# Weight loads of an attention kernel: five transfers at once, or six parts over six tiles

## The chip, the cores and the metric

The kernel runs on one core of a Trainium2 chip. The metric is the device time of one execution in microseconds (us), the median of several runs. The profile comes from one execution, taken by the hardware profiler. A kilobyte (KB) is 1024 bytes.

## The reference

One layer on x of 2048 rows by 256: attention with 16 heads of 128, and then a mixture of experts. Every projection matrix is stored as codes with one scale per block of 32 rows.

```
w  = codes * repeat(scales, 32, axis=0)        # wq, wk, wv: 256 x 2048; wo: 2048 x 256
q, k, v = ln(x) @ w + bias                     # 16 heads of 128
attn = softmax(q k^T / sqrt(128)); out = attn @ v
x = x + ln(out @ wo + bo)
x = x + ln(top-2 of 8 experts: silu(x Wg) * (x Wu) @ Wd)
```

## The kernel before

The attention stage is one loop over 256 steps, `g = 16 * h + t`: head `h` and tile `t`, a block of 128 query rows. The order of the instructions on each engine is the order of the program text; the framework adds only the semaphore waits.

In one tile, the steps are these.

- TensorE multiplies Q by K^T for the 2048 keys in two halves (L453 to L457). Every operand is split into a high and a low float16 part, so three products stand for one.
- VectorE takes the row maxima (L458), and ScalarE the exponential with its row sums (L469).
- VectorE forms the reciprocal of the row sum (L479, once per tile), and ScalarE writes the normalized high part `ph` (L483).
- VectorE writes the low part `pl` in two halves (L498), from `p`, `m` and `ph`.
- SP, the queue of the sync engine, transposes `ph` (L486) and `pl` (L502) into `pt` with one DMA each. There are two buffers of `pl`, three of `ph`, and two of `pt`, each for four tiles.
- TensorE multiplies V by `pt` (L517 to L519), some six tiles later: `PVLAG` counts in half tiles. After four tiles the result `o` is scaled by ScalarE, split into two float16 parts by POOL (GpSimd, L531 and L532) and written to `ot_d` in DRAM by POOL's DMA queue (L533, 256 KB). This comes in tiles 2, 6, 10 and 14 of each head.

Between these, `fill` projects Q, K and V of the coming heads, a piece in each tile: ScalarE takes a piece out of PSUM (L204, L235), and POOL splits it (L205 and L206, L236 and L237). POOL works through its queue in order, so that a split of tile t often runs in tile t + 1.

The weights are used in pairs of heads, p = h // 2: 256 columns of `wq`, `wk` and `wv` each. `load_w` brings one of them: four transfers of 64 KB for the scales, each row repeated over 32 partitions (L130), and one of 256 KB for the codes (L135), all issued on POOL's queue, into the tiles `st_s` and `st_c`, of which there is one each. `dequant` scales the scales (L152) and multiplies (L154) on POOL. For pair p + 1 this goes on in the even head of pair p: V, K and Q are loaded in tiles 0, 3 and 6, at the beginning of the tile, and dequantized in tiles 2, 5 and 8. Odd heads load nothing.

In head 14, the last even one, three of the eight loads of `wo` take the place of these: `load_wo` in tiles 7, 10 and 13 issues four transfers of scales on ScalarE's queue (L571) and the codes on SP's (L576); `dequant_wo` (L584) follows in tiles 9, 12 and 15. The other five come in head 15, from `late`. After the attention stage come the output projection and the experts.

Of the kernel before, what the change touches and what calls it, by code (L numbers as in the profile page):

```python
# [8 lines left out]
F32 = mybir.dt.float32  # L9
# [12 lines left out]
D = 256  # L22
NH = 16
# [14 lines left out]
def sandwich(  # L38
# [22 lines left out]
    nc = tc.nc  # L61
# [53 lines left out]
    stage = proj_ctx.enter_context(tc.tile_pool(name="stage", bufs=1, side="right"))  # L115

    W = {}
    raw = {}

    def load_w(p, which, pool, eng, sbufs=1):  # L120
        codes, scales = {
            "q": (wq_codes, wq_scales),
            "k": (wk_codes, wk_scales),
            "v": (wv_codes, wv_scales),
        }[which]
        cols = bass.ts(p, 256)
        sc = pool.tile([128, 2, 256], F32, name="st_s", bufs=sbufs)
        sv = scales.rearrange("(kc b) n -> b kc n", b=4)
        for b in range(4):
            eng.dma_start(  # L130
                out=sc[32 * b : 32 * b + 32],
                in_=sv[b : b + 1, :, cols].to_broadcast([32, 2, 256]),
            )
        cd = pool.tile([128, 2, 256], F32, name="st_c", bufs=sbufs)
        eng.dma_start(  # L135
            out=cd, in_=codes.rearrange("(kc p) n -> p kc n", p=128)[:, :, cols]
        )
        raw[(p, which)] = (sc, cd)

    IX = {"q": 0, "k": 1, "v": 2}  # L140

# [6 lines left out]
    def dequant(p, which):  # L148
        sc, cd = raw.pop((p, which))
        f = sig[:, 2, IX[which] : IX[which] + 1]  # L150
        if p > 0:
            nc.gpsimd.tensor_scalar(sc, sc, f, 1.0, ALU.mult, ALU.mult)  # L152
        w = wpool.tile([128, 2, 256], BF, name="w" + which)
        nc.gpsimd.tensor_tensor(w, cd, sc, ALU.mult)  # L154
        W[(p, which)] = w
# [18 lines left out]
    def flush():  # L174
        while pending:
            pending.pop(0)()
# [32 lines left out]
    def proj_v(p, t0, n, tag="pj", wide=None):  # L209
        w = W[(p, "v")]  # L210
        ps = proj_psum(tag)
        for j in range(n):
            i = 0
            for kc in range(2):
                for hl in range(2):
                    nc.tensor.matmul(
                        ps[:, bass.ts(j, 256)], xnT[:, t0 + j, hl * 2 + kc, :],
                        w[:, kc, :], start=(i == 0), stop=(i == 3),
                    )
                    i += 1  # L220
        if t0 % 4 == 0:
            V[(p, t0 // 4)] = kqv.tile([128, 2, 4, 256], HP, name="v", bufs=7)
        v = V[(p, t0 // 4)]
        sl = slice(t0 % 4, t0 % 4 + n)
        psv = ps[:, : n * 256].rearrange("p (t d) -> p t d", d=256)
        if wide is None:
            nc.scalar.copy(v[:, 0, sl, :], psv)
            pending.append(lambda: nc.vector.tensor_tensor(
                v[:, 1, sl, :], psv, v[:, 0, sl, :], ALU.subtract
            ))  # L230
        else:
            t32 = wide.tile([128, 512], F32, name="t32")[:, : n * 256].rearrange(
                "p (t d) -> p t d", d=256
            )
            nc.scalar.copy(t32, psv)  # L235
            nc.gpsimd.tensor_copy(v[:, 0, sl, :], t32)  # L236
            nc.gpsimd.tensor_tensor(v[:, 1, sl, :], t32, v[:, 0, sl, :], ALU.subtract)  # L237

    with tc.tile_pool(name="start", bufs=4) as st:
# [9 lines left out]
        for i, scales in enumerate((wq_scales, wk_scales, wv_scales)):  # L249
            nc.scalar.dma_start(  # L250
                out=smax[:, i], in_=scales.rearrange("b (c n) -> (b c) n", n=128)
            )
        for i, bias in enumerate((bq, bk, bv)):
            nc.scalar.dma_start(
                out=b48[16 * i : 16 * i + 16], in_=bias.rearrange("(h p) -> h p", p=128)
            )
        cds = {}
        for i, (which, codes, scales) in enumerate(
# [3 lines left out]
            cd = st.tile([128, 2, 256], F32, name="cd0", bufs=3)  # L262
            nc.sync.dma_start(
                out=cd, in_=codes.rearrange("(kc p) n -> p kc n", p=128)[:, :, 0:256]
# [182 lines left out]
    def scores_half(h, t, half, m):  # L447
        q = Q[(h, t // 4)]
        qc = bass.ts(t % 4, 128)
        s = s_pair()  # L450
        for j in range(2):
            k = K[(h, 2 * half + j)]
            nc.tensor.matmul(s[:, j, :], q[:, 0, qc], k[:, 0, :], start=True, stop=False)  # L453
            nc.tensor.matmul(s[:, j, :], q[:, 0, qc], k[:, 1, :], start=False, stop=False)  # L454
        for j in range(2):
            k = K[(h, 2 * half + j)]
            nc.tensor.matmul(s[:, j, :], q[:, 1, qc], k[:, 0, :], start=False, stop=True)  # L457
        nc.vector.tensor_reduce(m[:, half : half + 1], s, AX.XY, ALU.max)  # L458
        return s
# [15 lines left out]
    def recip(m):  # L475
        nc.vector.tensor_scalar(
            m[:, 5:6], m[:, 3:4], m[:, 4:5], 1.0 / PS, ALU.add, ALU.mult
        )
        nc.vector.reciprocal(m[:, 6:7], m[:, 5:6])  # L479
# [76 lines left out]
    def pv_unit(u):  # L556
        n, e = divmod(u - PVLAG, 8)
        if 0 <= n < 4 * NH:
            pv_part(n // 4, n % 4, 2 * e, 2 * e + 2)
# [3 lines left out]
    so = wo_scales.rearrange("(h b) n -> b h n", b=4)  # L563
    co = wo_codes.rearrange("(h p) n -> p h n", p=128)
    wo_raw = {}

    def load_wo(j, pool, tags, bufs):
        hs = slice(2 * j, 2 * j + 2)
        sc = pool.tile([128, 2, D], F32, name="wos", tag=tags[0], bufs=bufs)
        for b in range(4):  # L570
            nc.scalar.dma_start(  # L571
                out=sc[32 * b : 32 * b + 32],
                in_=so[b : b + 1, hs].to_broadcast([32, 2, D]),
            )
        cd = pool.tile([128, 2, D], F32, name="woc", tag=tags[1], bufs=bufs)
        nc.sync.dma_start(out=cd, in_=co[:, hs])  # L576
        wo_raw[j] = (sc, cd)

    def dequant_wo(j):
        sc, cd = wo_raw.pop(j)  # L580
        if j % 4 == 0:
            wo.append(kqv.tile([128, 8, D], BF, name="wo", tag="v", bufs=7))
        hs = slice(2 * (j % 4), 2 * (j % 4) + 2)
        nc.gpsimd.tensor_tensor(wo[j // 4][:, hs], cd, sc, ALU.mult)  # L584
# [43 lines left out]
    def load_oi(b, half, j, tag="kT"):  # L628
        oi = kqv.tile(
            [128, 4, 2, 256], HP, name="oi", tag=tag, bufs={"kT": 8, "v": 7}[tag]  # L630
        )
        nc.sync.dma_start(
            out=oi, in_=ot_d[b][:, 4 * j : 4 * j + 4, :, bass.ts(half, 256)]
        )
        OIN[(b, half, j)] = oi
# [40 lines left out]
    for g in range(NS + 2):  # L676
        h, t = divmod(g, NT)
        live = g < NS
        if live:
            if t in (0, 3, 6) and h % 2 == 0 and h + 2 < NH:  # L680
                load_w(h // 2 + 1, "vkq"[t // 3], stage, nc.gpsimd)
            m = small.tile([128, 8], F32, name="m", bufs=6)
            s0 = scores_half(h, t, 0, m)
            if g == 0:
                proj_v(0, 0, 2)
                proj_v(0, 2, 2, "pv")
        if g == NS:
            load_oi(0, 1, 1)
            load_oi(0, 1, 2)
            load_oi(0, 1, 3)  # L690
        if prev is not None:
            recip(prev[2])
        if prev2 is not None:
            low_half(1, *prev2)
        flush()
        if defer:
            pv_unit(2 * g - 1)
            defer = False
        pv_unit(2 * g)
        if prev is not None:  # L700
            prev = (*prev, high_part(*prev))
        if live:
            s1 = scores_half(h, t, 1, m)
            negmax(m)
            p = softmax((s0, s1), m)
        if prev is not None:
            low_half(0, *prev)
        prev2 = prev
        first = live and (2 * g + 1 - PVLAG) % 8 == 0
        if not first:  # L710
            pv_unit(2 * g + 1)
        if live:
            fill(h, t)
        if first and h == NH - 1:
            defer = True
        elif first:
            pv_unit(2 * g + 1)
        if live:
            prev = (h, t, m, p)
        else:  # L720
            prev = None
        if h % 2 == 0 and t in (2, 5, 8) and h + 2 < NH:
            dequant(h // 2 + 1, "vkq"[t // 3])
        if h == 0 and t in (8, 9):
            tail_consts(t - 8)
        if h == NH - 2 and t in (7, 10, 13):
            load_wo((t - 7) // 3, stage, ("st_s", "st_c"), 1)
        if h == NH - 2 and t in (9, 12, 15):
            dequant_wo((t - 9) // 3)
        if h == NH - 1:  # L730
            late(t)
        if g == NS:
            X1[0] = kqv.tile([128, 4, D], F32, name="x1_0", tag="kT", bufs=8)
            nc.sync.dma_start(out=X1[0], in_=XV[:, 0])
# [377 lines left out]
    for q in range(4 * NCH + 2):  # L1112
        b, c = divmod(q, NCH)
# [61 lines left out]
```

## Time and profile before

| | us |
|---|---|
| median of 3 runs | 1877.07 |
| lowest and highest | 1873.67 and 1882.77 |
| the profiled execution | 1879.05 |
| its span, first to last instruction | 1877.3 |
| the loop over heads: first and last `L479` | 38.9 and 1588.5 |

The page of the profile gives for each engine the busy time, its share of the span and the number of instructions. Its digits are busy tenths in 40 slices of the span. The share of the DMA engines can pass 1.00, since packets overlap. In a row of the timeline, a transfer that an engine issues has the time that the issue took, not the time to its landing. A wait is told as "engine, line <- what ended it: us in total, times, longest". In a table of stretches, each row is a stretch of time with the busy time of each engine and its number of instructions, the granted clock of TensorE, the DMA share, and GB/s.

### The profile page before, as it was taken

The numbers are of one execution on the slowest core, as the hardware profiler recorded it, in microseconds if no ns is written. First come the engines' busy times: TensorE is split into PE (matmuls) and PEld (weight loads), VectorE is DVE, ScalarE is ACT, GpSimd is POOL, SyncE is SP. The second block draws the span as 40 slices with busy tenths as digits, with TensorE's granted clock in tenths as the row PEclk, the third lists the DMA queues.
The fourth block names the chain that finished last, engine by engine and source line by source line (L and its number), as shares of the span: only waits on it lengthen the run. The fifth ranks groups of instructions, "written<-read, shape, count | busy, mean of one in ns | idle before, by whom it ended". The sixth has DMA issues, their size and how long they took to land. (4 is left out here: it accounts for less than half of the span.)

```text
span 1877.3 us, 25533 instructions
## 1 busy us (share of the span) xinstructions
PE 1794.1 (96%) x8890; PEld 936.0 (50%) x8890; DVE 1632.4 (87%) x2267; ACT 1365.5 (73%) x1730; POOL 907.5 (48%) x893
## 2 busy tenths in 40 slices
PE   7899999999999999999999999999999988899998
PEld 4344444444444444444444444444444434588887
DVE  7999989998999899998999999889999886458566
ACT  5888878888888788887888888778888776123232
POOL 3554574457544654465445644564444342233222
PEclk9999999999999999999999999999999999999999
DMA  3999999999999999999999999999999999982121
GB/s 91 190 193 190 189 202 198 190 189 202 196 191 189 193 195 191 192 201 193 188 190 205 197 189 192 183 202 194 191 186 205 208 220 219 259 236 69 55 71 57
DMA packets 1133345, 342.31 MB, mean 182 GB/s; under 512 B 1070896, under 2 KB 1120768, under 8 KB 1133216
## 3 DMA queue, kind: packets, MB, share of 16 engines
q1 hardware_dynamic: 1120528, 310.53, 90.4%
q0 software_dynamic: 9584, 27.82, 5.9%
q10 hardware_dynamic: 3104, 2.33, 0.5%
q8 instruction: 70, 1.15, 0.2%
q14 instruction: 59, 0.48, 0.1%
HBM read 53.22 MB, written 18.94 MB: 38 GB/s over the span
## 5 line engine op out<-in xcount | busy, mean ns | idle before, releaser
L498 DVE SCALAR_TENSOR_TENSOR pl<-p,m,ph 128x1024 f16<-128x1024 f32 x512 | 731.6, 1429 | 50.2 <-DMA pt<-pl 43.9
L469 ACT ACTIVATE p<-s,m,ssc 128x1024 f32<-128x1024 f32 x512 | 611.9, 1199 | 192.6 <-DVE m L462 158.9
L458 DVE TENSOR_REDUCE m<-s 128x1 f32<-128x1024 f32 x512 | 622.0, 1215 | 23.2 <-PE s L457 22.7
L483 ACT ACTIVATE ph<-p,m 128x2048 f16<-128x2048 f32 x256 | 513.0, 2004 | 84.7 <-issue 30.2
L518 PE MATMUL pv<-pt,v 128*128 128x512 f16 x1024 | 391.2, 382 | 27.9 <-DMA pt<-pl 27.9
L453 PE MATMUL s<-kT,qT 128*128 128x512 f16 x1024 | 389.9, 381 | 16.9 <-ACT p L469 13.9
L517 PE MATMUL pv<-pt,v 128*128 128x512 f16 x1024 | 390.6, 381 | 7.4 <-DMA pt<-ph 5.3
L519 PE MATMUL pv<-pt,v 128*128 128x512 f16 x1024 | 391.2, 382 | 0.0
L454 PE MATMUL s<-kT,qT 128*128 128x512 f16 x1024 | 389.8, 381 | 0.0
L457 PE MATMUL s<-kT,qT 128*128 128x512 f16 x1024 | 305.3, 380 | 0.0
L205 POOL CAST qT<-t 128x512 f16<-128x512 f32 x63 | 86.4, 1371 | 247.2 <-ACT t L204 247.2
L236 POOL CAST v<-t 128x256 f16<-128x256 f32 (+1 forms) x105 | 54.3, 517 | 271.8 <-ACT t L235 271.8
L518 PEld LDWEIGHTS <-v 128*128 128x128 f16 x1024 | 100.7, 98 | 153.8 <-issue 29.4
L454 PEld LDWEIGHTS <-qT 128*128 128x128 f16 x1024 | 100.4, 98 | 135.2 <-issue 33.4
L517 PEld LDWEIGHTS <-v 128*128 128x128 f16 x1024 | 100.6, 98 | 130.8 <-issue 7.0
L519 PEld LDWEIGHTS <-v 128*128 128x128 f16 x1024 | 100.7, 98 | 123.6 <-issue 7.6
L457 PEld LDWEIGHTS <-qT 128*128 128x128 f16 x1024 | 100.5, 98 | 121.8 <-issue 1.7
L453 PEld LDWEIGHTS <-qT 128*128 128x128 f16 x1024 | 100.6, 98 | 111.3 <-issue 3.2
L237 POOL TENSOR_TENSOR v<-t,v 128x256 f16<-128x256 f32 (+1 forms) x105 | 146.8, 1398 | 8.4
L928 POOL TENSOR_TENSOR hh<-sg,hh 128x512 fp32r<-128x512 f32 x42 | 54.5, 1298 | 144.6 <-ACT hh L927 99.4
L927 ACT CAST hh<-sg 128x512 fp32r<-128x512 f32 (+1 forms) x45 | 27.5, 611 | 118.4 <-DVE sg L939 118.4
L206 POOL TENSOR_TENSOR kT<-t,kT 128x512 f16<-128x512 f32 x60 | 107.8, 1796 | 5.0
(184 smaller groups left out, 2019.4 us busy)
## 6 DMA issues: line engine op xcount, KB each, us to landing
oi<-ot_d SPq DMA_DIRECT2D x32, 512.0 KB, 6.9
ot_d<-o POOLq DMA_DIRECT2D x63, 256.0 KB, 4.1
pt<-ph SPq DMA_TRANSPOSE x256, 5.1
pt<-pl SPq DMA_TRANSPOSE x256, 4.7
cu<-ct_d SPq DMA_DIRECT2D x16, 256.0 KB, 3.9
xt<-in_L_attn_x SPq DMA_DIRECT2D x4, 512.0 KB, 5.6
wos<-in_L_attn_wo_scales ACTq DMA_DIRECT2D x32, 64.0 KB, 4.5
woc<-in_L_attn_wo_codes SPq DMA_DIRECT2D x8, 256.0 KB, 3.5
```

Of the source, the lines that this page charges most:

```text
L206: nc.gpsimd.tensor_tensor(t[:, 1, :], t32, t[:, 0, :], ALU.subtract)
L237: nc.gpsimd.tensor_tensor(v[:, 1, sl, :], t32, v[:, 0, sl, :], ALU.subtract)
L453: nc.tensor.matmul(s[:, j, :], q[:, 0, qc], k[:, 0, :], start=True, stop=False)
L454: nc.tensor.matmul(s[:, j, :], q[:, 0, qc], k[:, 1, :], start=False, stop=False)
L457: nc.tensor.matmul(s[:, j, :], q[:, 1, qc], k[:, 0, :], start=False, stop=True)
L458: nc.vector.tensor_reduce(m[:, half : half + 1], s, AX.XY, ALU.max)
L469: nc.scalar.activation(p[:, bass.ts(i, 1024)], s, AF.Exp, bias=m[:, 2:3], scale=ssc[:, 0:1], accum_out=m[:, 3 + i : 4 + i],)
L483: nc.scalar.activation(ph, p, AF.Copy, scale=m[:, 6:7])
L498: nc.vector.scalar_tensor_tensor(pl[:, cs], p[:, cs], m[:, 6:7], ph[:, cs], ALU.mult, ALU.subtract)
L517: nc.tensor.matmul(ps, vh, d[:, :, c, :], start=(c == 0), stop=False)
L518: nc.tensor.matmul(ps, vh, d[:, :, 16 + c, :], start=False, stop=False)
L519: nc.tensor.matmul(ps, vl, d[:, :, c, :], start=False, stop=(c == 15))
```

## The change

`load_w` issues one of six parts: four parts are the scales, 64 KB each, and two the codes, 128 KB each, since the codes are now loaded in two halves. `weight_steps`, at the end of a tile, says which part comes in which tile. In an even head, K comes in tiles 0 to 5 and Q in tiles 8 to 13, dequantized in tiles 7 and 15. In an odd head, V comes in tiles 3 to 8, dequantized in tile 10, for the pair after the next head's. Head 0 has a plan of its own: V in tiles 1 and 2 (three parts each), K in tiles 6 to 11, Q in tiles 14 and 15 (three parts each).

The three loads of `wo` in head 14 also go to POOL's queue, in three parts: two of 128 KB (two transfers each) and the codes with 256 KB, in tiles 4 to 6, 8 to 10 and 12 to 14; they are dequantized in tiles 8 and 12, and tile 0 of head 15. Nothing else differs; the instructions of TensorE and VectorE are the same and in the same order.

```diff
-    def load_w(p, which, pool, eng, sbufs=1):
+    def load_w(p, which, piece):
...
-        for b in range(4):
-            eng.dma_start(
-                out=sc[32 * b : 32 * b + 32],
-                in_=sv[b : b + 1, :, cols].to_broadcast([32, 2, 256]),
-            )
-        cd = pool.tile([128, 2, 256], F32, name="st_c", bufs=sbufs)
-        eng.dma_start(
-            out=cd, in_=codes.rearrange("(kc p) n -> p kc n", p=128)[:, :, cols]
-        )
-        raw[(p, which)] = (sc, cd)
+        if piece == 0:
+            raw[(p, which)] = (
+                stage.tile([128, 2, 256], F32, name="st_s"),
+                stage.tile([128, 2, 256], F32, name="st_c"),
+            )
+        sc, cd = raw[(p, which)]
+        if piece < 4:
+            sv = scales.rearrange("(kc b) n -> b kc n", b=4)
+            nc.gpsimd.dma_start(
+                out=sc[32 * piece : 32 * piece + 32],
+                in_=sv[piece : piece + 1, :, cols].to_broadcast([32, 2, 256]),
+            )
+        else:
+            kc = piece - 4
+            nc.gpsimd.dma_start(out=cd[:, kc], in_=codes[bass.ts(kc, 128), cols])
+
+    def weight_steps(h, t):
+        if h % 2 == 1:
+            v_at, p = 3, (h + 3) // 2
+        else:
+            v_at, p = None, h // 2 + 1
+        if p >= NH // 2:
+            return
+        if h == 0:
+            plan = {
+                1: ("v", (0, 1, 2)), 2: ("v", (3, 4, 5)), 14: ("q", (0, 1, 2)),
+                15: ("q", (3, 4, 5)),
+            }
+            plan.update({6 + i: ("k", (i,)) for i in range(6)})
+            done = {5: "v", 13: "k"}
+        elif v_at is None:
+            plan = {i: ("k", (i,)) for i in range(6)}
+            plan.update({8 + i: ("q", (i,)) for i in range(6)})
+            done = {7: "k", 15: "q"}
+        else:
+            plan = {v_at + i: ("v", (i,)) for i in range(6)}
+            done = {v_at + 7: "v"}
+        if h == 1 and t == 1:
+            dequant(1, "q")
+        if t in plan:
+            which, pieces = plan[t]
+            for i in pieces:
+                load_w(p, which, i)
+        if t in done:
+            dequant(p, done[t])
...
+    def load_wo_part(j, part):
...
+        if part < 2:
+            for b in (2 * part, 2 * part + 1):
+                nc.gpsimd.dma_start(
+                    out=sc[32 * b : 32 * b + 32],
+                    in_=so[b : b + 1, hs].to_broadcast([32, 2, D]),
+                )
+        else:
+            nc.gpsimd.dma_start(out=cd, in_=co[:, hs])
...
-            if t in (0, 3, 6) and h % 2 == 0 and h + 2 < NH:
-                load_w(h // 2 + 1, "vkq"[t // 3], stage, nc.gpsimd)
...
-        if h % 2 == 0 and t in (2, 5, 8) and h + 2 < NH:
-            dequant(h // 2 + 1, "vkq"[t // 3])
+        if live:
+            weight_steps(h, t)
...
-        if h == NH - 2 and t in (7, 10, 13):
-            load_wo((t - 7) // 3, stage, ("st_s", "st_c"), 1)
-        if h == NH - 2 and t in (9, 12, 15):
-            dequant_wo((t - 9) // 3)
+        if h == NH - 2 and t in (8, 12):
+            dequant_wo(t // 4 - 2)
+        if h == NH - 1 and t == 0:
+            dequant_wo(2)
+        if h == NH - 2 and t >= 4 and t % 4 < 3:
+            load_wo_part(t // 4 - 1, t % 4)
```

## The prediction

> **What bounds the kernel now.** First the page. TensorE is busy 96% and VectorE 87%, but the page says that pipelined matmuls overstate TensorE, and the DMA row stands at 9 for the whole attention stage. No average answers for one stage, so the second view is the table of stretches, cut at the head boundaries: the 16th `L479` (one per tile) of each head.
>
> ```profile
> PE 1794.1 (96%) x8890; PEld 936.0 (50%) x8890; DVE 1632.4 (87%) x2267; ACT 1365.5 (73%) x1730; POOL 907.5 (48%) x893
> DMA  3999999999999999999999999999999999982121
> ```
>
> ```profile
> core 0: us, PE busy (x) PEld busy (x) DVE busy (x) ACT busy (x) POOL busy (x), PEclk, DMA share, GB/s
> 322.41:416.72 94.31, 94.12 (x452) 44.05 (x451) 90.38 (x113) 79.80 (x100) 45.36 (x44) 1.00 1.05 191
> 416.72:514.41 97.69, 93.97 (x448) 43.35 (x446) 89.06 (x113) 80.22 (x99) 62.59 (x63) 1.00 1.12 198
> 514.41:608.72 94.31, 94.11 (x452) 44.02 (x450) 90.38 (x113) 79.80 (x100) 45.37 (x44) 1.00 1.07 190
> 608.72:708.45 99.73, 95.14 (x448) 43.89 (x446) 88.52 (x113) 80.14 (x99) 61.55 (x63) 0.98 1.07 194
> ```
>
> These are heads 3 to 6. Odd heads load no weights: each takes 94.31 (VectorE busy 90.38; its idle time ends on ScalarE). Even heads carry three loads and take 98.05, 97.69, 99.73, 99.01, 97.12 and 100.80 (heads 2 to 12): 592.4 against 6 x 94.31, an **excess of 26.5 us**, with VectorE *less* busy. What it waits for is in the waits of head 2 (224.36 to 322.41):
>
> ```profile
> DVE pl L498 <- DMA pt<-pl: 5.5, 4, 2.1
> PE pv L518 <- DMA pt<-pl: 3.6, 3, 1.6
> ```
>
> Neither line exists in head 3. The late thing is the transpose of the probabilities. Tile 0 of head 4, POOL's queue and then SP's, and SP's of the same tile of head 5:
>
> ```profile
> 418.71 2.16 POOL L130 DMA_DIRECT2D st_s<-in_L_attn_wv_scales  x4
> 420.87 0.73 POOL L135 DMA_DIRECT2D st_c<-in_L_attn_wv_codes  x1
> ```
>
> ```profile
> 420.99 4.72 SPq L486 DMA_TRANSPOSE pt<-ph  x1
> ```
>
> ```profile
> 518.21 2.10 SPq L486 DMA_TRANSPOSE pt<-ph  x1
> ```
>
> Five issues put 512 KB on the DMA engines within 2.9 us; the next transpose holds SP 4.72 us instead of 2.10. The two `pl` buffers then come free late and VectorE stops, or TensorE lacks `pt`, one or two tiles later.
>
> A stall can cost twice. Half-clock stretches follow TensorE gaps: here a wait of 2.02 us for `pt` from 647.6, and two of 1.4 us from 1199.85:
>
> ```profile
> 649.00:653.00 4.00, 3.39 (x9) 1.29 (x10) 2.29 (x3) 3.31 (x6) 3.71 (x6) 0.57 1.02 193
> 1202.00:1206.00 4.00, 2.98 (x8) 1.12 (x9) 2.73 (x4) 2.74 (x6) 0.00 (x0) 0.57 1.11 237
> ```
>
> They lie in heads 6 and 12, the two longest, at tiles of 7.83 and 8.14 us (5.9 is usual).
>
> **What the Trainium skill says.** "DMA: Bandwidth & Descriptors", Queues, rings and completion order: a DMA engine takes turns between queue rows, a packet at a time, so a load on POOL's queue slows SP's transposes; the trace agrees (4.72 against 2.10). "SBUF — State Buffer", SBUF: two separate sides: VectorE (with two SBUF inputs) and GpSimd share a port pair by an exclusive lock, and whoever starts first blocks the other. The trace agrees for splits: at 528.75 `L498` takes 2.04 instead of 1.27 because `L532` started at 528.55. It shows no such price for a DMA issue: `L498` of tile 0 takes 1.28 in head 4 among five issues and 1.27 in head 5 among none. "TensorE: Matmul & The Clock Gate", What's actually happening: after an idle window of about 3.4 us the clock is halved; the stretches above (0.57) agree.
>
> **The change part by part.**
>
> *Bursts removed.* Per pair of heads three loads of 512 KB become 18 parts of 64 or 128 KB in 18 of 32 tiles. Can a tile take a part? A tile lasts 5.9 us on average; the two transposes of an undisturbed tile hold SP 2.17 + 2.10 = 4.3. Summed over SP's rows in the timeline, transposes hold SP 78 us in an odd head and 92 in an even one, 14 / 3 = 4.7 us per 512 KB: 0.6 per 64 KB, 1.2 per 128 KB, inside the 1.6 of slack. From the landing of a `pl` transpose to the next write of its buffer, tiles 3, 7 and 11 of the odd heads show 1.8 to 2.9 us in reserve. And the 256 KB of `ot_d` in every fourth tile stalls nothing in odd heads. So I take the burst stalls as gone: **-26.5**, half-clock stretches included. What limits next is VectorE, as in the odd heads.
>
> *Where parts still meet.* In the instruction order of the changed program the 128 KB part of tile 5 (and of 13) stands directly ahead of `L531` to `L533` of tile 6 (14): 384 KB within some 3 us, three quarters of a burst. A burst costs 26.5 / 18 = 1.5. Two meetings in each of six even heads; bounds 0 (the reserve holds) to 1.1 each, 13 in all. I take 0.5: **+6**.
>
> *Dequants moved* (tiles 2, 5, 8 to 7, 15 and, for V, odd tile 10): same 1.66 + 1.27 us on POOL, which is 48% busy. They can block `L498` for at most what a split does, 2.04 - 1.27 = 0.77; at tile 9 of head 0 one runs and the tile takes its usual 5.65. Bounds 0 to 0.77 for 18 dequants; I take 0.2: **+3.6**. Each follows its last part by two tiles, some 11 us, and landings take at most 8.9 in this trace: no wait. First use is tiles later still (K: tile 2 of the next head; V: tile 9 of the next even head), so nothing queued behind a dequant is urgent.
>
> *Issues added.* POOL gets 21 more for Q, K and V and 15 for `wo`: 36 x 0.55 = 20 us over the stage, hidden by POOL's idle half and, as shown, free for VectorE. Queued behind them are the splits `L205` to `L237`, whose consumers are four tiles away in the case of Q. Four of the eight `o` splits of a pair start 0.55 to 0.73 later, behind a part; `L498` may then take the port first and save up to 0.6. Bounds: -14 (24 splits at 0.6) to +5 (a quarter of them shifted into a block of 0.77); I take **-3**.
>
> *Head 14.* Three `wo` loads leave ACT's queue (12 x 0.45 us) and SP's (three) for POOL, in 128, 128 and 256 KB; the 256 KB part shares tiles 6, 10, 14 with `ot_d`. The head takes 97.54 now; bounds 0 to -4; I take **-1.5**. Its last dequant moves past the head's end to tile 0 of head 15: POOL is idle there. *Head 0:* V in two tiles, Q in tiles 14 and 15 stay near-bursts; -1.5 to +1.5, taken **0**.
>
> Sum: -26.5 + 6 + 3.6 - 3 - 1.5 = **-21.4**. The profiled execution took 1879.05 (span 1877.3), so 1857.7; it lies 2.0 above the median of 1877.07. Forecast **1856**.
>
> **The rivals.** That the change does not do what it says is excluded by the instruction order: the parts stand in different tiles, and TensorE's and VectorE's orders are as before. *The stall moves into odd heads.* They have no excess now because nothing is loaded there; if each part costs its share of a burst (1.5 / 6 = 0.25), nothing or a few us are saved: 1868 to 1879. For it: DMA share is 1.05 even in odd heads, so the engines are never idle. Against: `ot_d`, two to four parts' worth, costs no stall.
>
> *Slower: port blocks.* Each part shifts the POOL work behind it by 0.55 to 0.73 us. If that puts a split just ahead of an `L498`, VectorE, the bound of the undisturbed tile, loses 0.77. There are 108 parts in heads 1 to 12; above 26.5 / 0.77 = 34 bad shifts the gain is gone, with 55 the time is 1877 - 26.5 + 42 = 1893. Against: VectorE starts first in most tiles, and the shift of `o` is in the good direction.
>
> *All of it returns and more:* no meetings, splits favourable: -26.5 - 10 - 2 gives 1838 to 1845.
>
> **How the numbers follow.** Under 0.5% (9.4 us) a measurement can hardly tell from no change. Forecast case (1846 to 1871) 0.68; full return 0.10; stall moved 0.14; slower 0.08. Range **1845 to 1874**: it reaches over half of the moved stall and leaves out its other half (0.07), the slower rival (0.08) and the far end of full return (0.05). Faster by over 0.5% (below 1867.7) takes the full return and most of the forecast case: **0.75**; within 0.5% **0.17**; slower **0.08**.
>
> **What would show it.** Right: even heads near 95, odd heads at 94 to 95, the waits of `L498` and `L518` for `pt` small in head 2 and its like, transposes of 2 to 3 us beside the parts, no half clock in heads 6 and 12. `L498` above its 1429 ns mean would show port blocks; odd heads above 96 with `pt` waits, the moved stall; a stall left at tiles 6 and 14, the meetings. Wrong: even heads still at 97 or more, or VectorE busy above 92 in a head.

## The result, and the profile after

The changed kernel takes 1874.56 us (median of 20 runs, 1868.37 to 1882.63), the kernel before in the same series 1885.47 (1873.67 to 1892.82). The ratio of the two means is 0.9951, with a 95% interval of 0.9933 to 0.9969: 0.49% faster, some 9 us. The forecast was a fall of 21 us, to 1856, with 1845 to 1874 as its range. The profiled execution after took 1870.90 us, with a span of 1869.1 against 1877.3.

The page after, its line of the engines and that of the DMA engines:

```profile
PE 1785.9 (96%) x8890; PEld 933.7 (50%) x8890; DVE 1628.8 (87%) x2267; ACT 1366.5 (73%) x1730; POOL 937.8 (50%) x929
DMA  2999999999999999999999999999999999982121
```

Apart from POOL's 36 added issues (x929, x893 before) nothing here tells of a change. The stretches do, again heads 3 to 6, cut at the reciprocals (now `L512`):

```profile
324.85:419.40 94.55, 93.93 (x452) 43.97 (x451) 90.46 (x113) 79.95 (x100) 54.40 (x54) 1.00 1.06 192
419.40:516.79 97.39, 93.46 (x448) 43.32 (x446) 87.93 (x112) 80.09 (x99) 55.66 (x56) 1.00 1.10 195
516.79:614.59 97.80, 95.70 (x452) 44.33 (x450) 90.41 (x113) 79.95 (x100) 52.65 (x54) 0.98 1.07 186
614.59:709.89 95.30, 93.21 (x448) 43.48 (x446) 87.78 (x112) 80.25 (x99) 56.15 (x56) 1.00 1.07 199
```

Even heads are shorter, but head 4 still takes 97.39, and odd heads, which took 94.31 each, have become longer: 97.80 in head 5. Summed over heads, with the two profiles against each other: even heads 2 to 12 fall by 15.5 us (592.4 to 576.9), odd heads 1 to 13 rise by 9.2 (660.1 to 669.3), head 14 falls by 3.2, and heads 0 and 15 rise by 1.0 together. That is the 8.5 us that the loop lost.

The waits of head 2, the head of the prediction's lines:

```profile
DVE m L491 <- PE s L490: 6.0, 9, 2.5
PE pv L551 <- DMA pt<-pl: 3.4, 3, 2.1
DVE pl L531 <- DMA pt<-pl: 1.0, 1, 1.0
```

VectorE's own wait for `pl` fell from 5.5 to 1.0, but TensorE's wait for `pt` stayed (3.6 before), and VectorE now waits for TensorE's scores behind it (1.1 before). Over heads 1 to 12 it is the same: VectorE waits 12.9 us for `pl` (21.1 before), TensorE 21.9 for `pt` (15.9) and VectorE 31.2 for scores (13.4). The stall is not gone; more of it now begins at TensorE. Its place is tile 14 of the even heads, 6.21 us when undisturbed and 7.50 on average now (9.36 and 8.71 in heads 2 and 4, 6.64 to 6.91 in the others), and tile 10 of the odd heads, 6.94 on average over heads 1 to 13. In head 4 the queues show this, SP's first and then POOL's:

```profile
499.09 3.70 SPq L535 DMA_TRANSPOSE pt<-pl  x1
502.89 3.81 SPq L519 DMA_TRANSPOSE pt<-ph  x1
506.79 3.13 SPq L535 DMA_TRANSPOSE pt<-pl  x1
```

```profile
499.77 0.59 POOL L141 DMA_DIRECT2D st_c<-in_L_attn_wq_codes  x1
504.42 0.58 POOL L141 DMA_DIRECT2D st_c<-in_L_attn_wq_codes  x1
507.16 0.57 POOL L566 DMA_DIRECT2D ot_d<-o  x1 [0.30 <-POOL o L565]
```

None of these transposes holds SP as long as the 4.72 us of a burst, but three in a row are late, one behind the other. The first one landed only 7.97 us after its issue (the median of the `pl` transposes is 5.03); a 128 KB part had been issued 0.68 us behind it. A first matmul of TensorE then waits 2.61 us for this transpose, and VectorE 1.76 for the buffer of `pl`. It landed at 507.06, before `ot_d` (`L566`) was issued: this stall is made by parts and transposes, without this tile's write of `o`. The half clock follows elsewhere, at 314 (tile 14 of head 2) and 581 (tile 10 of head 5):

```profile
314.00:318.00 4.00, 4.00 (x12) 1.51 (x11) 1.54 (x2) 1.67 (x3) 2.37 (x4) 0.57 1.30 194
580.50:584.50 4.00, 4.00 (x13) 1.46 (x11) 1.55 (x3) 1.00 (x3) 2.76 (x4) 0.57 1.11 204
```

### The profile page after: what moved, and what is told of

Same layout as the page of the kernel before. It is cut to its first block, busy times and chain, and to the rows that moved or that the text cites. A ratio compares the mean times of both kernels' runs of the same rounds, so it can differ in the third digit from the quotient of the medians.

```text
span 1869.1 us, 25550 instructions
## 1 busy us (share of the span) xinstructions
PE 1785.9 (96%) x8890; PEld 933.7 (50%) x8890; DVE 1628.8 (87%) x2267; ACT 1366.5 (73%) x1730; POOL 937.8 (50%) x929
## 5 line engine op out<-in xcount | busy, mean ns | idle before, releaser
L531 DVE SCALAR_TENSOR_TENSOR pl<-p,m,ph 128x1024 f16<-128x1024 f32 x512 | 723.6, 1414 | 34.5 <-DMA pt<-pl 32.6
L238 POOL CAST qT<-t 128x512 f16<-128x512 f32 x63 | 81.8, 1299 | 241.8 <-ACT t L237 241.8
L269 POOL CAST v<-t 128x256 f16<-128x256 f32 (+1 forms) x105 | 45.9, 437 | 285.7 <-ACT t L268 285.7
L270 POOL TENSOR_TENSOR v<-t,v 128x256 f16<-128x256 f32 (+1 forms) x105 | 156.9, 1494 | 8.5
L239 POOL TENSOR_TENSOR kT<-t,kT 128x512 f16<-128x512 f32 x60 | 97.7, 1628 | 5.1
```

Of the source, the lines that this page charges most:

```text
L239: nc.gpsimd.tensor_tensor(t[:, 1, :], t32, t[:, 0, :], ALU.subtract)
L531: nc.vector.scalar_tensor_tensor(pl[:, cs], p[:, cs], m[:, 6:7], ph[:, cs], ALU.mult, ALU.subtract)
```

## The experiments

The theories: **DMA** (the parts still come in the way of the transposes, whose reserve is smaller than the prediction took it) and **port** (the moved dequants start just ahead of an `L531` and block VectorE). "Heads 1 to 12" is the time from the last reciprocal of head 0 to that of head 12: 1158.2 us before, 1151.2 after. It comes from one profile of each kernel.

| run | us | ratio to before (95%) | heads 1 to 12 |
|---|---|---|---|
| changed, again | 1872.76 | 0.9950 (0.9936 to 0.9965) | 1149.2 |
| e1, dequants moved | 1865.98 | 0.9909 (0.9880 to 0.9938) | 1144.2 |
| e2, changed, no loads | 1854.75 | 0.9847 (0.9812 to 0.9882) | 1130.8 |
| e3, order of parts | 1870.41 | 0.9927 (0.9899 to 0.9955) | 1147.4 |
| e4, parts twice | 1913.28, one execution | | 1189.8 |
| e5, before with wo parts | 1891.93, one execution | | 1173.7 |
| e6, bursts in the new places | 1877.49, one execution | | 1155.5 |
| e7, e1 and e3 | 1865.99 | 0.9916 (0.9902 to 0.9930) | 1145.4 |
| e8, before, no loads | 1846.02, one execution | | 1123.9 |
| e9, e1 with gaps | 1865.95 | 0.9916 (0.9890 to 0.9943) | 1141.6 |
| e10, changed, no ot_d | 1858.42, one execution | | 1136.3 |
| e11, e1, no loads | 1843.71, one execution | | 1120.8 |

### What the transfers cost: e2 and e8

```diff
+        first = (p, which) == (1, "v")
...
+        raw[(p, which)] = kept[0]
+        if not first:
+            return
...
-            nc.gpsimd.tensor_scalar(sc, sc, f, 1.0, ALU.mult, ALU.mult)
+            st = stage.tile([128, 2, 256], F32, name="st_t")
+            nc.gpsimd.tensor_scalar(st, sc, f, 1.0, ALU.mult, ALU.mult)
+            sc = st
```

> The changed kernel, with only the first V load issued: every later dequant of Q, K and V reads that one tile again and writes its product of scales to a tile of its own, so the weights of later heads are wrong and 120 of 126 parts are left out. Dequants stand where they stood. It gives the price of the transfers. Theory DMA: the stalls at tile 14 of even heads (7.5 now, on average) and tile 10 of odd heads (6.9) go, heads 1 to 12 fall from 1151 to about 1137 us, no wait of L531 or L551 for pt is left there; tile 0 of odd heads stays at 6.44. Theory port: heads 1 to 12 stay above 1146, since the dequants are still there.

> The kernel before with only the first V load issued; all later dequants read that tile and write the scales' product to a tile of their own, so later weights are wrong and 20 of 21 loads are left out. It gives the price of the bursts without the dequants. If the excess of even heads is the transfers' (theory DMA), they fall from 98.7 on average to 93.5 to 94.5 and no wait of L498 or L518 for pt is left; heads 1 to 12 near 1131. If the dequants carry part of it (theory port), even heads stay above 95.5.

Without loads no wait for `pt` is left in head 2 of e2, and tile 14 takes 6.21 again. Heads 3 and 4 of e2, and then of e8:

```profile
316.17:411.21 95.04, 94.34 (x450) 43.90 (x449) 91.34 (x112) 79.89 (x100) 50.25 (x48) 1.00 1.03 190
411.21:504.62 93.41, 93.33 (x450) 43.73 (x448) 89.78 (x112) 79.83 (x99) 48.30 (x44) 1.00 1.06 190
```

```profile
316.04:410.39 94.35, 94.24 (x453) 44.09 (x451) 90.60 (x112) 79.84 (x100) 45.43 (x44) 1.00 1.07 192
410.39:503.27 92.88, 92.79 (x447) 43.54 (x445) 89.05 (x112) 79.95 (x99) 54.51 (x48) 1.00 1.07 190
```

So the transfers cost 1158.2 - 1123.9 = 34.3 us before, and 1151.2 - 1130.8 = 20.4 after. The difference of the two floors is the dequants' new places: 1130.8 - 1123.9 = +6.9. The sum, -13.9 + 6.9 = -7.0, is the change in heads 1 to 12. Neither theory alone carries it. Whole executions, which do not hang on one profile, say about the same: without its loads the kernel before takes 35.5 us less than the median of its own series (1881.55 - 1846.02), the changed kernel 18.0 less (1872.76 - 1854.75, medians of two series). Both floors lie lower than expected (1137 and 1131). The even heads of e8 take 92.9, one 93.4: an undisturbed even head is shorter than an odd one, which the prediction used as its floor.

### Is the spreading itself the gain: e6

```diff
-            plan = {i: ("k", (i,)) for i in range(6)}
-            plan.update({8 + i: ("q", (i,)) for i in range(6)})
+            plan = {0: ("k", range(6)), 8: ("q", range(6))}
...
-            plan = {v_at + i: ("v", (i,)) for i in range(6)}
+            plan = {v_at: ("v", range(6))}
```

> The changed kernel with the six parts of a load of heads 1 to 12 issued in one tile again (K in even tile 0, Q in even tile 8, V in odd tile 3), dequants where the changed kernel has them. It undoes the spreading alone. If the spreading makes the gain, each of 18 bursts costs what it cost before (31.3 / 18 = 1.74 us over the kernel without loads): heads 1 to 12 at 1131 + 31 = 1162 us, odd heads with V near 97. If the gain comes from the new places of loads and dequants, heads 1 to 12 stay at or below 1153.

1155.5, between the two: 24.7 us over e2, 1.37 per burst, against 34.3 / 18 = 1.9 in the old places. The parts cost 20.4 (18.5 in the second profile). On these single profiles some 10 us of the transfers' gain go with the new places (other tiles, the end of a tile and not its beginning, V in odd heads) and 4 to 6 with the spreading. How far that can be trusted is shown by e5, whose heads 1 to 12 have the loads of the kernel before: they took 1173.7 against 1158.2. Bursts differed by 15 us between two executions, the parts by 2. That the spreading is worth little is therefore only indicated.

### Is the reserve used up: e4 and e10

```diff
...
+            again = stage.tile([128, 256], F32, name="st_3", bufs=1)
+            nc.gpsimd.dma_start(out=again, in_=codes[bass.ts(kc, 128), cols])
```

> The changed kernel with each of the 126 parts issued a second time into a tile that nobody reads (10.5 MB more). If a tile's reserve is as large as the prediction took it (1.6 us of slack against 0.6 to 1.2 per part), the time grows by less than 10 us. If the reserve is used up already (theory DMA), it grows by the price of a burst for every 512 KB, 21 x 1.5 = 31 us, or more, up to the time that 512 KB hold SP, 21 x 4.6 = 97 us. VectorE busy time per head stays within 1 us of the changed kernel (an issue does not take the port).

The span grew by 42.4 us (1911.5), heads 1 to 12 by 38.6: the second helping costs nearly twice the 20.4 us of the first. A few of POOL's issues also waited for an earlier copy to land (one 4.0 us in head 2), so a part of this is not the transposes'. VectorE was busy 91.57 in head 3 and 89.91 in head 4, 1.1 and 2.0 more than after, against the expectation. The issues are not the reason: over heads 1 to 12 VectorE is busy 1073.7 us after, 1079.1 with twice the issues and 1086.2 in e2, which has no parts there. One `pl` write takes 1414, 1417 and 1441 ns on average in the three.

```diff
-            nc.gpsimd.dma_start(out=ot_d[b][:, h], in_=o)
+            if h >= 11:
+                nc.gpsimd.dma_start(out=ot_d[b][:, h], in_=o)
...
-            out=oi, in_=ot_d[b][:, 4 * j : 4 * j + 4, :, bass.ts(half, 256)]
+            out=oi, in_=ot_d[b][:, 11:15, :, bass.ts(half, 256)]
```

> The changed kernel without the writes of o to ot_d in heads 0 to 10 (the output projection reads heads 11 to 14 four times, so the output is wrong); parts and dequants as they are. If the parts cost time because ot_d has used up the reserve of every fourth tile (theory reserve), the price of the transfers in heads 1 to 11, 1055.0 - 1037.3 = 17.7 us, falls below 4, and those heads take at most 1041 us. If a part has its own price wherever it stands (0.19 us each), they stay above 1052.

Heads 1 to 11 of e10 in one stretch:

```profile
130.17:1171.58 1041.41, 1032.55 (x4928) 481.66 (x4926) 983.99 (x1233) 878.81 (x1095) 587.12 (x565) 1.00 1.05 187
```

1041.4, 0.4 above the expected bound, with all parts in place; two half-clock stretches are in it. The price fell from 17.7 to 4.1 us. It is read against e2, whose floor has `ot_d` in it; undisturbed tiles are alike in both (tile 10 of odd heads: 6.21). By heads the result is not one but two. In the odd heads 1 to 11 the parts cost 4.6 us after, and here the time falls to 4.2 below e2's: nothing is left at tile 10, and the gain of tiles 6 and 7 (below) stays. In the even heads 2 to 10 they cost 13.0 after and still 8.3 here, 7.6 of it in heads 6 and 10, with one long stall each. That of head 10, SP and then POOL:

```profile
1057.61 3.21 SPq L535 DMA_TRANSPOSE pt<-pl  x1
1060.92 4.41 SPq L519 DMA_TRANSPOSE pt<-ph  x1
```

```profile
1058.31 0.58 POOL L141 DMA_DIRECT2D st_c<-in_L_attn_wq_codes  x1
```

The first landed after 8.15 us, TensorE waited 2.71 us for it, and the tile took 10.42, with no write of `o` in the whole head. It is the picture of head 4 after: a 128 KB part 0.7 us behind a `pl` transpose. In head 6 it is 0.33 us, landing after 7.06. Not every such meeting costs: in head 3 after, a part 0.75 us behind a `pl` transpose let it land after 5.81.

The issue times of the `pl` transposes fall too, but not to the floor (least, median, most, in ns); after, e2 and e10:

```profile
L535 SPq DMA_TRANSPOSE pt<-pl x256: 1685/2798/5504, 45.4 to 1596.3; - x128
```

```profile
L542 SPq DMA_TRANSPOSE pt<-pl x256: 1616/1999/6004, 45.2 to 1577.1; - x128
```

```profile
L535 SPq DMA_TRANSPOSE pt<-pl x256: 1653/2380/6085, 45.3 to 1584.6; - x128
```

Before, the median was 2198: in the changed kernel the typical transpose is slower. In the odd heads it is parts and `ot_d` together that use up the reserve; in the even heads, which have twice the parts, parts alone now and then do.

### The dequants: e1 and e11

```diff
+        if h % 2 == 1 and h > 1 and t == 0 and (h + 1) // 2 < NH // 2:
+            dequant((h + 1) // 2, "q")
...
-            done = {7: "k", 15: "q"}
+            done = {}
...
-            done = {v_at + 7: "v"}
+            done = {12: "v"}
...
+        if h % 2 == 0 and h > 0 and t == 8:
+            dequant(p, "k")
```

> The changed kernel with its dequants moved in POOL's queue: K from even tile 7 to tile 8, Q from even tile 15 to tile 0 of the next head, V from odd tile 10 to tile 12, so that each follows a split of Q and starts some 3.0 us into the tile. Loads as in the changed kernel. Theory port (a dequant that starts just ahead of L531 blocks VectorE): tile 0 of odd heads 3 to 13 falls from 6.44 to 5.82 (-3.7 us in all), tiles 7 to 8 of even heads and 10 to 11 of odd ones give 0.3 each time: -6 to -8 us against the changed kernel, ratio to before about 0.991. Theory DMA (what is left is transfers in the way of the transposes): those tiles change by less than 0.1, ratio stays near 0.995.

> The kernel with moved dequants, with only the first V load issued (later weights wrong, as in e2). It gives the price of the dequants at their new places. Theory port: tile 0 of odd heads at 5.82 and heads 1 to 12 near 1124 us, as in the kernel before without loads, against 1131 in the changed kernel without loads. If the places of the dequants do not matter by themselves: 1131.

Tile 0 of head 5 in the changed kernel, POOL and VectorE, and then VectorE of e1, in which Q's dequant waits for the split of `qT`:

```profile
518.83 0.68 POOL L185 TENSOR_SCALAR st_s<-st_s,sig 128x512 f32<-128x512 f32 x1
519.59 1.26 POOL L187 TENSOR_TENSOR wq<-st_c,st_s 128x512 bf16<-128x512 f32 x1
```

```profile
519.67 2.27 DVE L531 SCALAR_TENSOR_TENSOR pl<-p,m,ph 128x1024 f16<-128x1024 f32 x1
```

```profile
516.11 1.27 DVE L535 SCALAR_TENSOR_TENSOR pl<-p,m,ph 128x1024 f16<-128x1024 f32 x1
```

`L187` starts 0.08 us ahead, and the write takes 2.27 us instead of 1.27; the tile takes 6.44, in e1 again 5.82. Heads 1 to 12 fall by 7.0 us (5.0 against the second profile of the changed kernel), the ratio to 0.9909, both much as theory port expected. The places agree only in part: over the six odd heads 1 to 11, tile 0 gives 2.9 us and tiles 10 and 11 give 4.0, but tiles 7 and 8 of even heads give nothing, and tiles 6 and 7 of odd heads lose 6.8, against gains elsewhere. Without loads (e11) the floor is 1120.8, 10.0 below the changed kernel's and 3 below that of the kernel before. The transfers cost 1144.2 - 1120.8 = 23.4 in e1, near the 20.4 of the changed kernel: the two causes are separate.

### Other plans: e3, e7, e9

```diff
...
+            mix = (0, 4, 1, 5, 2, 3)
-            plan = {i: ("k", (i,)) for i in range(6)}
+            plan = {i: ("k", (mix[i],)) for i in range(6)}
...
+            mix = (4, 0, 1, 5, 2, 3)
```

> The changed kernel with the same parts in the same tiles in another order: K and Q as scales, codes, scales, codes, scales, scales; V as codes, scales, scales, codes, scales, scales. Before tile 14's ot_d stand two parts of 64 KB, not two of 128. Theory DMA, in the form that 128 KB parts meet ot_d: tile 14 of even heads falls from 7.5 to 6.3, tile 10 of odd heads from 6.9 to 6.4, and about 6 to 8 us go in all, ratio to before about 0.991. If only the sum of bytes counts, or port blocks: no change beyond 2 us, ratio near 0.995.

> Moved dequants (as in e1) and mixed order of the parts (as in e3) together. If the two causes add, heads 1 to 12 fall from 1151 by the 7 us of e1 and the 4 us of e3 to 1140, ratio to before 0.987 to 0.989. If one uses up the other's gain, the ratio stays at 0.991.

Tile 10 of odd heads fell to 6.34, tile 14 of even heads only to 7.06, and tile 8 rose from 6.04 to 6.37. Heads 1 to 12 fell by 3.8 and the ratio to 0.9927, between what the two cases expected (6 to 8 us, and 2 at most). With 64 KB parts ahead of it tile 14 is still late: that points to the run of six parts, more than to the size of the last two. Together with e1 nothing was added (1145.4 against 1144.2).

```diff
-            plan = {i: ("k", (i,)) for i in range(6)}
-            plan.update({8 + i: ("q", (i,)) for i in range(6)})
+            at = {0: (0, 1), 3: (2, 3), 4: (4,), 7: (5,)}
+            plan = {i: ("k", at[i]) for i in at}
+            plan.update({8 + i: ("q", at[i]) for i in at})
```

> The kernel with moved dequants (K tile 8, Q tile 0 of the next head, V tile 12) and another plan: of six parts, two scales in tile 0, two in tile 3, codes in tiles 4 and 7 (K; Q eight tiles later; V: scales in 3 and 4, codes in 7 and 8), so that no part is issued directly ahead of ot_d. If what is left is the reserve being drained where parts and ot_d come in the same two tiles, tile 14 of even heads falls from 6.83 to below 6.4, and heads 1 to 12 from 1144 to below 1139, ratio to before near 0.988. If only the sum of bytes over a run of tiles counts, they stay at 1142 to 1146; if pairs of parts already act as bursts, they rise above 1147.

1141.6 lies between the bounds of the first two cases (1139 and 1142). The average of tile 14, 6.92, is that of one head: head 4 takes 10.05, the other five 6.00 to 6.74, where e1 has 5.80 to 7.37. The gaps took the usual stall out of tile 14 and left a rare long one, again with a 128 KB part 0.8 us behind a `pl` transpose, which landed after 7.81. The whole time hardly shows it (0.9916, e1 0.9909), since other tiles rose, tile 6 of odd heads to 6.59. So e9 does not decide between its cases.

### The wo parts, and the changed kernel again: e5, r_after_again

> The kernel before with only the three wo loads of head 14 in parts; Q, K and V in bursts as before. If this part of the change works by itself, heads 14 and 15 together fall from 205.9 to about 203.6 us, as in the changed kernel, half of it perhaps the half-clock stretch that head 14 has before; the rest of the trace stays. If it is without effect, they stay within 1 us of 205.9.

> The changed kernel once more, on the chip of the next three: ratio to before 0.993 to 0.997. Its second profile says how far the 20.4 us that transfers cost in heads 1 to 12 of the first are luck: by theory DMA the places of the stalls are the same (tile 14 of even heads, tile 10 of odd ones above 6.5), and heads 1 to 12 lie within 5 us of 1151.

The edit of e5 is the diff's `load_wo_part` and its four lines in the loop, on the kernel before. Heads 14 and 15 took 95.6 + 108.2 = 203.7, as expected; the execution is slower as a whole because of its bursts. But one profile does not carry this: with the same `wo` parts these two heads took 205.8 in the second profile of the changed kernel, and 202.8 to 206.1 in the experiments; without them 205.9 twice (before and e8). A gain of the `wo` parts is not shown. In heads 1 to 12 the second profile repeats the first: tile 14 at 7.37, tile 10 at 6.56, 1149.2.

## Why the prediction was wrong in size

**Right.** The bound, the cause of the excess and the direction. VectorE's waits for `pl` became fewer (12.9 us in heads 1 to 12, 21.1 before), not none; DMA issues on POOL cost VectorE nothing (busy 90.46 in head 3, 90.38 before). Head 0 gave +0.1 (taken: 0). Head 14 gave -3.2 (taken: -1.5, bounds to -4), but the second profile does not repeat it: there heads 14 and 15 together take 205.8, and 205.9 before. `o` splits behind a part help: tiles 6 and 7 of odd heads 1 to 11 are 3.9 us below e2 in all (taken: -3 for all splits).

**The step that failed** is "Can a tile take a part?", and with it the two terms that rest on it: -26.5 for bursts that are gone, and +6 for the meetings. The net was -20.5. The runs showed -13.9 for the transfers, -10.0 if the 3.9 of the `o` splits is taken out. The bursts cost more than was taken (34.3; the floor was set by odd heads, at 94.31, where e8 shows 92.9), but of it 20.4 + 3.9 = 24.3 came back, not 6. The 1.6 us of slack was read from one quiet pair of transposes, in a tile without `ot_d`. The same paragraph had the better number: SP is held 78 us of 94.3 in an odd head, 1.0 us of room per tile, and six parts in a row ask for 0.6 to 1.2 each. e10 shows whose room it was: without `ot_d` the price falls from 17.7 to 4.1 us, and at tile 10 of the odd heads nothing is left. That `ot_d` alone stalls nothing does not mean that a part beside it stalls nothing. The meetings were also looked for at the wrong pair: the long stall of tile 14 in head 4 comes before that tile's `ot_d`, with a 128 KB part right behind a `pl` transpose, and e10 and e9 each have one like it. Why some of these meetings cost 2.5 to 4.2 us and others nothing stays open; the half clock is a part of it in some heads (last section).

**The dequants** were taken at +3.6 and cost +6.9, inside the bounds. Five tiles 0 of odd heads give 0.62 each (3.2 with head 1's 0.1); as much lies in even heads, chiefly tiles 10 and 11, where the old place of Q's dequant had held `o` back in VectorE's favour. In tile 10 of head 4 VectorE's write starts 0.28 us ahead of the split of `o` in e8 and takes 1.28, and 0.19 behind it in e2, where it takes 2.04. No run moved this alone.

**The rival of the moved stall** was half right: odd heads did rise, by 9.2 us. By the tile times of heads 1 to 11, the dequants' blocking is 3.6 of it, stalls at tiles 10 and 11 are 7.1, and the near-burst at the end of head 0 is 0.8, in tile 0 of head 1; tiles 6 and 7 take 3.9 back. The rival of blocked ports was right as a mechanism: dequants, not the parts, did the blocking.

**The base** moved as well: the first three runs had a median of 1877.07, and 20 have 1885.47. The burst kernel spreads over 19 us; the profile explained was one of its faster executions. On the old base the same ratio would have given 1867.9: the fall is 9 us there too, and not 21.

**A version that beats both** is e1: parts as in the changed kernel, dequants behind a split of Q. 0.9909 (0.9880 to 0.9938) against 0.9951 (0.9933 to 0.9969); these intervals still meet, but e7, which has the same dequants, lies clear of the changed kernel in one series: 0.9916 (0.9902 to 0.9930) against 0.9950 (0.9936 to 0.9965).

## What to carry to other kernels

A tile's room for another transfer is better judged by an average over many tiles, with every transfer that already stands there, than by its quietest tile: take the resource's held time over a whole period (here 78 of 94.3 us). Look also at what a part is issued right behind. When work is moved on GpSimd's queue, look at what VectorE starts next: 0.1 us ahead or behind decides who waits for whom. And measure the floor, with the suspected transfers left out, on both sides of a change; here the two floors differed by 6.9 us, as much as heads 1 to 12 gained in all (7.0).

## What the runs showed of the hardware

- A DMA issue on POOL leaves VectorE alone: the mean `pl` write is 1414 ns after, 1417 with every part issued twice (e4) and 1429 before. GpSimd's two-input operation does not: it took 1.00 us from one `L531`.
- Whether a half-clock stretch follows a gap of TensorE depends on where the gap falls. In each profile all these stretches start whole multiples of 3.413 us apart (after: 65.37, 314.54 and 580.78 lie 73 and 78 multiples apart), as if time were cut into steps of 3.413 us. From the first reciprocal to the end of head 14, the 14 profiles have 29 such stretches; in the step right before each, TensorE is idle for 1.9 to 3.4 us in all, and no other step at full clock has more than 1.96. So the gap of 2.06 us at 311.5 after, inside one step, was followed by a half clock; that of 2.61 us at 504.6 was not, for a border at 505.7 cuts it into 1.1 and 1.5. The prediction named an idle window of 3.4 us; here 2 us of it were enough. Up to head 13 there were three stretches before, three and one in the two profiles of the changed kernel, and none in e2 or e6.
- The stalls of the same bursts differed by 15 us between two executions (1158.2 before and 1173.7 in e5, heads 1 to 12), while heads without loads repeat within 0.1 us (94.31 and 94.35).
- In four long stalls (heads 2 and 4 after, head 10 of e10, head 4 of e9) a 128 KB load had been issued 0.7 to 0.8 us behind a 512 KB transpose on another queue, which then landed after 7.25 to 8.15 us; the median is about 5. The same meeting in head 3 after ended at 5.81, so it is not the whole cause.
